# Four fused convolution layers: weights and tables of the small U-net layers loaded once for all groups, with one fold-table buffer fewer

## The chip, the cores and the metric

The kernel runs on one NeuronCore of a Trainium2 chip. A core has four compute engines that run their own instruction streams in order: TensorE (PE, matrix products; PEld is its weight load), VectorE (DVE), ScalarE (ACT) and GpSimd (POOL). SyncE (SP) mostly issues DMA transfers. [...] The metric is the device time of one execution in microseconds (us).

## The reference

The input x is 16 images of 32 channels, 128 x 128, in f32. Four layers follow, each of the form x = x + layer(norm(x)), where the norm takes out mean and variance of pairs of channels.

```python
x = x + _L0_conv_ref(_gn(x), W2, b2, W1, b1)     # row LSTM along diagonals
x = x + _L1_conv_ref(_gn(x), weight)             # out = -sum |patch - w|, 3x3, quantised
x = x + _L2_conv_ref(_gn(x), weights1)           # Hartley transform, 32x32 modes mixed, back
x = x + _L3_conv_ref(_gn(x), ...)                # below

# layer 3
y = get_operator(x)               # five edge operators, each normalised: 160 channels
y = maxpool2(conv3x3(y, conv1))   # 128 -> 64
y = maxpool2(conv3x3(y, conv2))   # 64 -> 32
y = maxpool2(conv3x3(y, conv3))   # 32 -> 16
y = conv3x3(y, conv4)
y = conv3x3(deconv2x2(y, deconv1), conv5)   # 16 -> 32
y = conv3x3(deconv2x2(y, deconv2), conv6)   # 32 -> 64
y = conv3x3(deconv2x2(y, deconv3), conv7)   # 64 -> 128
return orig * y
```

## The kernel before

**Stages.** Stage 0 (layer 0, to about 687 us) runs alone. Then `Differences` makes layer 1 in 32 units (16 images, two halves each). A unit has 72 taps; a tap is one tile of 128 x 8192 values relu(q - w) in f16, made either by DVE (line 760, tile `d_dve`) or by ACT (line 757, tile `d_act`). PE sums each tap over channels (line 647, `acc`). The stage ends near 5616 us, with the last unit.

**Work in the background.** Layers 2 and 3 are made by `After`, in four groups of four images. `After.work` is a generator: `prepare` first, then for each group `forward` (the Hartley transform and the mixing of modes, line 1214), `encoder` (`back`, lines 1278 and 1323; `first_layers`; `small_layers`) and `last` (up7 and the output). Each `yield` tells a planner, `Weave`, what follows: a positive number is so many us of PE work, a negative one a planned wait (for a load, or for DVE), and `("after", 4g+3)` holds group g back until its last image has left layer 1. While `Differences` emits taps, `Weave.advance` emits as much of the generator's work as fits by planned times (a tap is taken as 2.36 us on DVE and 7.15 us on ACT). Whether a tap goes to DVE or ACT, and how many zero products `keep_busy` adds on PE, follows from the same planned times. `keep_order` then fixes that order on every engine.

**After the last unit.** Groups 0 to 2 run in the background of `Differences`, with their tiles on the left side of SBUF. What is left of them when the last unit ends is interleaved with group 3 by `drain`, again by planned times, with planned waits stretched by 1.5 until one of the two is left. Group 3 is done by `end`, a copy of `after` with its tiles on the right, where the layer 1 tiles were, and with more buffers: six for `e_v`.

**`prepare`.** It composes each deconvolution with the convolution that follows into one table (`up5`, `up6`, `up7`, class `Composed`, stored in `up_d`), and for each of the five edge operators a fold table, the `conv1` weights folded with the operator (line 1031 stores it by SP in `fold_d`, 128 x 2880 values; the stores are between 992 and 1325 us).

**`first_layers`.** For each group the mean and variance of the operators' outputs come from Gram products (`statistics`, line 1428). Then the fold tables are weighted with them into one tile of weights, `wf`: ten half tables `v` of 720 KB come by POOL's queue (line 1544), DVE scales the first two (line 1557) and adds the others (line 1559). The pool `e_v` has four buffers: the first four halves are issued inside `statistics`, each further one after the DVE instruction that uses up a buffer. Then `conv1` runs on `wf` (line 1745; the corrections at the picture's rim are line 1780, pooling is line 1672, spreading to the 32-channel layout line 1683), and `small_layers` is called for `conv2`, whose weights are loaded at line 1566.

**`small_layers`, second call.** It makes `conv3`, `conv4` (line 1595), `up5` and `up6` (line 905) of a group of four images. It begins with its loads: `replicated` brings `conv3`'s and `conv4`'s weights (four transfers of 36 KB each, by `by_rows`, line 342), `Composed.loaded` brings a table of 400 KB each for `up5` and `up6` (line 891), all on SP's queue, ten transfers a group; then comes `yield -7.0`. The tiles live in the pool `e_c`, which is opened and closed for each group. `last` loads `up7`'s table in the same way.

**Memory.** Per partition a half table `v` takes 5760 bytes, the weights of one small conv 1152, and one table of `Composed` 3200. POOL's queue has a ring in SBUF, `dynamic_dma_scratch_size`, of 4096 bytes.

Of the kernel before, what the change touches and what calls it, by code (L numbers as in the profile page):

```python
# [333 lines left out]
def by_rows(nc, tile, dram, store=False):  # L334

    for j in range(4):
        part = tile[32 * j : 32 * j + 32]
        rows = bass.AP(dram.tensor, dram.offset + j * dram.ap[0][0], [list(v) for v in dram.ap[1:]])
        if store:
            nc.sync.dma_start(rows, part)  # L340
        else:
            nc.sync.dma_start(part, rows)
# [8 lines left out]
class Weave:  # L351
# [10 lines left out]
    def __init__(self, work):  # L362
        self.work, self.pending = work, None
        self.pe = self.dve = self.act = self.now = self.base = 0.0
        self.until = self.ready = 0.0
        self.draining = self.alone = False
        self.stretch = 1.0
        self.finished, self.count, self.put_off, self.for_act, self.ends = -1, 0, [], [], {}
# [449 lines left out]
def replicated(nc, pool, src, n, name):  # L818

    wr = pool.tile([128, n, 32], F32, name=name)  # L820
    whole = bass.AP(src.tensor, src.offset, [[0, 4], [n * 32, 32], [1, n * 32]])
    by_rows(nc, wr.rearrange("p t o -> p (t o)"), whole)
    return wr
# [135 lines left out]
class After:  # L959


    def __init__(self, nc, tc, side, sm, ps, cst, bias, a, d, stat, out):
        self.nc, self.tc, self.side, self.ps, self.cst, self.bias = nc, tc, side, ps, cst, bias
        self.a, self.d, self.stat, self.out = a, d, stat, out
        self.spare, self.banks = None, 0
        self.sm, self.scales = sm, {}
        self.buffers = {"t_x": 4, "xm": 3, "xw": 2, "t_w": 3, "t_r": 4, "frames": 2, "gm": 5, "e_v": 4, "l_x": 2}
        store = [d["up"][i] for i in range(3)]
        self.up5 = Composed(nc, sm, a, "deconv1", "conv5", bias[:, 7:8], bias[:, 4:5], store[0])
        self.up6 = Composed(nc, sm, a, "deconv2", "conv6", bias[:, 8:9], bias[:, 5:6], store[1])  # L970
        self.up7 = Composed(nc, sm, a, "deconv3", "conv7", bias[:, 9:10], bias[:, 6:7], store[2])
# [25 lines left out]
    def prepare(self):  # L997

        nc, tc = self.nc, self.tc
        with self.pool("p_sm") as pool:  # L1000
            for up in (self.up5, self.up6, self.up7):
                yield from up.compose(pool, self.ps)
        with self.pool("f_sm") as pool:
            w1 = replicated(nc, pool, self.a["conv1"], 45, "w1")
            yield -20.0
            for k, op in enumerate(OPERATORS):
                t = pool.tile([128, 90, 32], F32, name="fold", bufs=2)
                nc.vector.memset(t, 0.0)
                src = w1[:, 9 * k : 9 * k + 9, :].rearrange("p (h w) o -> p h (w o)", w=3)
                for n, (th, tw, r0, c0, h, w, sign) in PARTS.items():  # L1010
                    at, const = PART_AT[n]
                    v = t[:, at : at + h * w, :].rearrange("p (h w) o -> p h (w o)", w=w)
                    for ur in range(3):
                        for uc in range(3):
                            rows = [i for i in th if 0 <= i + ur - r0 < h]
                            cols = [i for i in tw if 0 <= i + uc - c0 < w]
                            if not op[ur][uc] or not rows or not cols:
                                continue
                            r, c = rows[0] + ur - r0, cols[0] + uc - c0
                            dst = v[:, r : r + len(rows), 32 * c : 32 * (c + len(cols))]  # L1020
                            s = src[:, rows[0] : rows[-1] + 1, 32 * cols[0] : 32 * (cols[-1] + 1)]
                            nc.vector.scalar_tensor_tensor(dst, s, sign * op[ur][uc], dst, ALU.mult, ALU.add)
                            self.weave.dve += 0.25
                            yield -1.0
                    for i in th:
                        for j in tw:
                            nc.vector.scalar_tensor_tensor(
                                t[:, const], w1[:, 9 * k + 3 * i + j], -sign, t[:, const], ALU.mult, ALU.add
                            )
                yield SUMMED  # L1030
                nc.sync.dma_start(self.d["fold"][k], t.rearrange("p t o -> p (t o)"))

    def forward(self, g):

# [496 lines left out]
    def first_layers(self, g, fp, frames, y2):  # L1531
        nc, tc, weave = self.nc, self.tc, self.weave
        sides = fp.tile([128, H + 4, 4], F32, name="sides")
        ops = fp.tile([128, 2, 5], F32, name="ops")
        wf = fp.tile([128, 90, 32], F32, name="wf")
        b1 = fp.tile([128, 4], F32, name="b1")
        with self.pool("e_v", self.buffers["e_v"]) as pool:
            v = []

            def table():  # L1540

                k, half = len(v) // 2, len(v) % 2
                v.append(pool.tile([128, 45, 32], F32, name="v"))
                nc.gpsimd.dma_start(
                    v[-1].rearrange("p t o -> p (t o)"), self.d["fold"][k, :, 1440 * half : 1440 * half + 1440]
                )

            with self.pool("e_s") as es:
                yield from self.statistics(g, es, frames, sides, ops, lambda: [table() for _ in range(self.buffers["e_v"])])
            yield -0.5  # L1550
            for n in range(10):
                k, half = n // 2, n % 2
                for part, i in (((0, 81 - 45), 0), ((81 - 45, 45), 1)) if half else (((0, 45), 0),):
                    s = ops[:, i, k : k + 1]
                    to, t = wf[:, 45 * half + part[0] : 45 * half + part[1]], v[n][:, part[0] : part[1]]
                    if k == 0:
                        nc.vector.tensor_scalar(to, t, s, None, ALU.mult)
                    else:
                        nc.vector.scalar_tensor_tensor(to, t, s, to, ALU.mult, ALU.add)
                    weave.dve += 0.1 + 0.033 * (part[1] - part[0])  # L1560
                if len(v) < 10:
                    table()
                yield -1.2
        with self.pool("e_y1") as y1p:
            y1 = self.padded(y1p, 64, "y1")
            self.wc = {"conv2": replicated(nc, y1p, self.a["conv2"], 9, "w_conv2")}
            yield from self.conv1(g, y1p, frames, y1, sides, wf, b1)
            with self.pool("e_c2") as cp:
                yield from self.small_layers(cp, None, y1, y2)

    def small_layers(self, cp, rp, y1, y2):

        nc, tc, weave, bias = self.nc, self.tc, self.weave, self.bias
        wc = self.wc
        if not y1:
            for n in ("conv3", "conv4"):
                wc[n] = replicated(nc, cp, self.a[n], 9, f"w_{n}")
            up5, up6 = self.up5.loaded(cp), self.up6.loaded(cp)
            y3, y4, y5 = (self.padded(cp, n, f"y{i}") for n, i in ((16, 3), (16, 4), (32, 5)))
            self.y6 = y6 = self.padded(rp, 64, "y6")  # L1580
            yield -7.0

        def conv(src, n, name, evict):
            rows = min(n // 4, 512 // n)
# [468 lines left out]
```

## Time and profile before

Four runs took 6645.91, 6638.22, 6632.50 and 6645.64 us, median 6641.93. The profiled execution is the first.

| what | value |
|---|---|
| profiled execution | 6645.91 us, span 6644.1 us |
| stage 0, 0 to 687 us: PE / DVE / ACT busy | 465.8 / 561.5 / 513.3 us |
| taps, 687 to 5616 us: PE / DVE / ACT busy | 4036.2 / 4677.1 / 4745.5 us of 4929 |
| after the last tap, 5616 to 6644 us: PE / DVE / ACT busy | 833.2 / 312.5 / 177.0 us of 1028 |
| mean granted TensorE clock | 0.916 |
| `v` from `fold_d`, POOL's queue | 40 transfers of 720 KB |
| `w_conv`, SP's queue | 48 transfers of 36 KB |
| `u_conv`, SP's queue | 12 transfers of 400 KB |

How to read the profile: it is one execution. "Busy" leaves out waits and the issue of DMA. A group of instructions is given with its source line, its engine, the operation, the tile written and the tiles read, how many there are, and the idle time of the engine just before them with what ended it ("<-DVE d_dve L760" means that a DVE instruction of line 760 released it, "<-DMA v" that a transfer into `v` did, "<-issue" that no wait is seen). The page records most f32 matmuls of `conv1` twice: 25,600 records stand for 12,800 instructions. A clock of 1.0 would be full speed.

### The profile page before, as it was taken

What the parts mean: (1) busy time and instruction counts of PE and PEld (TensorE: products, weight loads), DVE (VectorE), ACT (ScalarE), POOL (GpSimd) and SP (SyncE); (2) the same over time, 40 slices, a digit from 0 to 9 for tenths busy, and PEclk for the clock granted to TensorE, in tenths of its full rate; (3) what the DMA queues carried; (4) which work ended last, traced back from release to release, by engine and by line L of the source; (5) the groups of instructions that cost most, each with busy time, mean ns of one, the idle gap of its engine ahead of it and who ended that gap; (6) DMA issues with size and microseconds to landing.
All of it is one profiled execution on the core that took longest, in us unless ns stands there. A gap on an engine that the chain in (4) does not pass through costs nothing.

```text
span 6644.1 us, 269240 instructions
## 1 busy us (share of the span) xinstructions
PE 5335.2 (80%) x126168; PEld 2775.4 (42%) x126168; DVE 5551.2 (84%) x6858; ACT 5435.8 (82%) x3191; POOL 70.0 (1%) x67
## 2 busy tenths in 40 slices
PE   3698677788777879997887879997877879887796
PEld 3675333334333433333333433333433434454584
DVE  7898899999999999998999999999999998242322
ACT  3898899999999999998999989999999998102112
POOL 0000000000000000000000000000000000000000
PEclk9999899999999989998989889998998889977897
DMA  7553322111344622212553732222553632347304
GB/s 317 212 190 118 79 58 62 53 45 47 75 137 124 195 83 72 56 45 57 118 156 95 214 105 61 56 56 50 123 153 91 196 114 72 119 142 210 94 27 108
DMA packets 380767, 728.06 MB, mean 110 GB/s; under 512 B 73284, under 2 KB 225348, under 8 KB 368772
## 3 DMA queue, kind: packets, MB, share of 16 engines
q1 hardware_dynamic: 372180, 676.41, 35.3%
q0 software_dynamic: 7040, 33.80, 1.5%
q8 instruction: 987, 16.17, 1.0%
q14 instruction: 128, 1.05, 0.1%
q10 hardware_dynamic: 432, 0.64, 0.0%
HBM read 510.69 MB, written 200.00 MB: 107 GB/s over the span
## 4 chain that ended last, share of the span: by engine, by line
issue 33%; PE 31%; DVE 20%; ACT 11%; DMA 3%; SPq 1%; POOL 0%; DVEq 0%; ACTq 0%; POOLq 0%
DVE d_dve L760 12%; PE acc L1745 11%; PE acc L647 9%; ACT d_act L757 8%; PE pg L223 3%; PE acc L905 3%; PE acc L1595 2%; ACT gt L237 2%; DVE y L1683 1%; ACT junk L198 1%; DVE stat L124 1%; PE acc L1428 1%; DVE pooled L1672 1%; DMA xm_d<-xm 1%; ACT th L247 1%
## 5 line engine op out<-in xcount | busy, mean ns | idle before, releaser
L757 ACT ACTIVATE d_act<-q,neg 128x8192 f16<-128x8192 f16 (+1 forms) x626 | 4428.3, 7153 | 164.9 <-PE acc L647 138.5
L760 DVE TENSOR_SCALAR d_dve<-q,qw 128x8192 f16<-128x8192 f16 (+1 forms) x1678 | 3870.8, 2361 | 180.3 <-PE acc L647 160.9
L647 PE MATMUL acc<-d_dve,sel 128*32 128x512 f16 x26848 | 1866.5, 401 | 456.2 <-DVE d_dve L760 353.2
L647 PEld LDWEIGHTS <-sel 128*32 128x32 f16 x36864 | 1003.3, 100 | 2096.7 <-issue 1428.4
L1745 PE MATMUL acc<-xp,wf 32*32 32x512 f32 x25600 | 986.8, 615 | 18.6 <-issue 14.9
L647 PE MATMUL acc<-d_act,sel 128*32 128x512 f16 x10016 | 723.8, 410 | 312.7 <-ACT d_act L757 296.9
L1745 PEld LDWEIGHTS acc<-xp,wf 32*32 32x32 f32 x25600 | 424.6, 104 | 379.6 <-issue 301.1
L1686 ACT ACTIVATE y<-pooled,b 32x128 f32<-32x128 f32 x456 | 182.4, 400 | 430.6 <-DVE pooled L1672 424.4
L905 PE MATMUL acc<-y,u_conv 32*32 32x256 f32 (+1 forms) x9728 | 342.5, 467 | 78.1 <-issue 59.9
L677 PE MATMUL acc<-q,zero 128*32 128x512 f16 x5676 | 402.9, 395 | 0.2 <-issue 0.2
L223 PE MATMUL pg<-h,wb 64*64 64x20 f32 (+15 forms) x8192 | 342.1, 305 | 60.8 <-DVE h L251 34.9
L237 ACT ACTIVATE gt<-pg,bias 128x20 f32<-128x20 f32 (+15 forms) x1024 | 331.7, 383 | 41.4 <-PE pg L223 39.4
L223 PEld LDWEIGHTS pg<-h,wb 64*64 64x64 f32 x8192 | 252.2, 150 | 136.1 <-DVE h L251 82.3
L1428 PE MATMUL acc<-xp 32*64 32x204 f32 (+3 forms) x8576 | 251.8, 345 | 53.8 <-issue 53.7
L905 PEld LDWEIGHTS acc<-y,u_conv 32*32 32x32 f32 x9728 | 154.5, 111 | 207.2 <-issue 158.3
L1844 ACT ACTIVATE xr<-xr,l_ms 128x1024 f32<-128x1024 f32 x64 | 68.7, 1146 | 209.5 <-DVE xr L1874 158.9
L1780 DVE TENSOR_TENSOR acc<-acc,cut 128x4 f32<-128x4 f32 x256 | 36.3, 165 | 234.6 <-PE acc L1745 231.9
L677 PEld LDWEIGHTS <-zero 128*32 128x32 f16 x5676 | 168.4, 100 | 152.3 <-issue 24.9
L1428 PEld LDWEIGHTS acc<-xp 32*64 32x64 f32 (+1 forms) x8576 | 171.2, 134 | 144.6 <-issue 139.6
L1373 ACT ACTIVATE xp<-xp,shift,stats 128x1280 f32<-128x1280 f32 (+1 forms) x64 | 91.5, 1434 | 161.2 <-DVE shift L1341 110.6
L1874 DVE SCALAR_TENSOR_TENSOR xr<-acc,l_one,xr 128x512 f32<-128x512 f32 x128 | 87.6, 743 | 155.8 <-PE acc L905 135.7
L223 PE MATMUL pg<-xn,wb 64*64 64x2 f32 (+63 forms) x4096 | 184.5, 290 | 24.5 <-issue 14.3
(217 smaller groups left out, 3739.9 us busy)
## 6 DMA issues: line engine op xcount, KB each, us to landing
q<-q_d SPq DMA_DIRECT2D x128, 536.2 KB, 9.6
xp<-xn_d SPq DMA_DIRECT2D x64, 660.0 KB, 4.9
xp<-x_d SPq DMA_DIRECT2D x56, 640.0 KB, 5.9
xr<-xn_d SPq DMA_DIRECT2D x64, 528.0 KB, 11.9
x_in<-in_x_dram SPq DMA_DIRECT2D x16, 2048.0 KB, 14.7
xn<-in_xs_dram SPq DMA_DIRECT2D x64, 512.0 KB, 7.0
res<-in_x_dram SPq DMA_DIRECT2D x64, 512.0 KB, 8.7
x_d<-res SPq DMA_DIRECT2D x64, 512.0 KB, 4.8
```

The lines of the kernel that those rows point to most:

```text
L223: nc.tensor.matmul(bank[c][q][64 * pair : 64 * pair + 64, :, :width], wb[half, 4 * kind + KIND[q]].rearrange("p b o -> p (b o)"), v[half], ...
L237: nc.scalar.activation(gt[:, q, :, :n], bank[c][q][:, :, :n], AF.Tanh if q == G else AF.Sigmoid, bias=bias[:, KIND[q] : KIND[q] + 1],)
L647: self.nc.tensor.matmul(acc[k][32 * j : 32 * j + 32, :], self.sel16[:, i // 9, :], d[:, row : row + 4, c : c + W], start=first, stop=last,)
L677: self.nc.tensor.matmul(acc[k][32 * j : 32 * j + 32, :], self.zero, q[:, :4, :W], start=False, stop=False)
L757: nc.scalar.activation(dst, src, AF.Relu, bias=self.neg[:, i : i + 1])
L760: nc.vector.tensor_scalar(dst, src, self.qw[:, i : i + 1], 0.0, ALU.subtract, ALU.max)
L905: nc.tensor.matmul(acc[blk][32 * j : 32 * j + 32, o : o + rows * n], t[part, 4 * par + tap, :], src[part, top : top + rows, left : left + ...
L1373: nc.scalar.activation(v, v, AF.Identity, bias=self.shift3, scale=self.stats3[:, 1])
L1428: nc.tensor.matmul(gram[blk][j : j + width, at : at + n], xp[part, l, 2 + j : 2 + j + width], xp[part, rows, j : j + width + 4], start=sta ...
L1595: nc.tensor.matmul(acc[blk][32 * j : 32 * j + 32, : rows * n], wc[name][part, tap, :], src[part, at : at + rows, kw : kw + n], start=tap == 0,
L1686: nc.scalar.activation(d, s, AF.Identity, bias=bj)
L1745: nc.tensor.matmul(acc[blk][32 * j : 32 * j + 32, :], tap_of("all", tap)[rows], xp[rows, 4 * j + kh : 4 * j + kh + 4, kw : kw + W], start= ...
```

## The change

- The weights of `conv3` and `conv4` and the tables of `up5` and `up6` are loaded at the end of `prepare` into the pool `sm`, which lives for the rest of the program: ten transfers on SP's queue, once, behind the store of the last fold table. All four groups use these tiles (`end` is a copy of `after` and shares them).
- `small_layers` has no loads of its own any more, and its planned wait is 1.0 in place of 7.0.
- `e_v` has three buffers for groups 0 to 2 in place of four. Group 3 keeps six.
- `dynamic_dma_scratch_size` is 2048 in place of 4096.

Per partition that is 8704 bytes more for the tables, 5760 less for `e_v` and 2048 less for the ring.

```diff
@@ After.__init__
-        self.buffers = {"t_x": 4, "xm": 3, "xw": 2, "t_w": 3, "t_r": 4, "frames": 2, "gm": 5, "e_v": 4, "l_x": 2}
+        self.buffers = {"t_x": 4, "xm": 3, "xw": 2, "t_w": 3, "t_r": 4, "frames": 2, "gm": 5, "e_v": 3, "l_x": 2}
@@ After.prepare, at its end
                 nc.sync.dma_start(self.d["fold"][k], t.rearrange("p t o -> p (t o)"))
+        self.wc = {n: replicated(nc, self.sm, self.a[n], 9, f"w_{n}") for n in ("conv3", "conv4")}
+        self.ups = self.up5.loaded(self.sm), self.up6.loaded(self.sm)
@@ After.first_layers
-            self.wc = {"conv2": replicated(nc, y1p, self.a["conv2"], 9, "w_conv2")}
+            self.wc["conv2"] = replicated(nc, y1p, self.a["conv2"], 9, "w_conv2")
@@ After.small_layers
         if not y1:
-            for n in ("conv3", "conv4"):
-                wc[n] = replicated(nc, cp, self.a[n], 9, f"w_{n}")
-            up5, up6 = self.up5.loaded(cp), self.up6.loaded(cp)
+            up5, up6 = self.ups
             y3, y4, y5 = (self.padded(cp, n, f"y{i}") for n, i in ((16, 3), (16, 4), (32, 5)))
             self.y6 = y6 = self.padded(rp, 64, "y6")
-            yield -7.0
+            yield -1.0
@@ kernel
-    nc = bacc.Bacc("TRN2", target_bir_lowering=False, num_devices=1, dynamic_dma_scratch_size=4096)
+    nc = bacc.Bacc("TRN2", target_bir_lowering=False, num_devices=1, dynamic_dma_scratch_size=2048)
```

The order of the built programs differs as follows. SP has 2346 instructions in place of 2376. DVE makes 1676 taps in place of 1678 and ACT 628 in place of 626. PE has 5860 zero products in place of 5676. All other counts are the same. The order is the same up to group 0's small layers, but for the ten loads and the fold-table reloads; from there the background work comes some taps earlier.

## The prediction

> **What bounds the kernel now.** I read the busy times first, then the table of stretches, then single pieces of the timeline at the two places where the change reorders work: the fold tables of groups 0 to 2, and the stretch after the last tap.
>
> ```profile
> PE 5335.2 (80%) x126168; PEld 2775.4 (42%) x126168; DVE 5551.2 (84%) x6858; ACT 5435.8 (82%) x3191; POOL 70.0 (1%) x67
> L757 ACT ACTIVATE d_act<-q,neg 128x8192 f16<-128x8192 f16 (+1 forms) x626 | 4428.3, 7153 | 164.9 <-PE acc L647 138.5
> L760 DVE TENSOR_SCALAR d_dve<-q,qw 128x8192 f16<-128x8192 f16 (+1 forms) x1678 | 3870.8, 2361 | 180.3 <-PE acc L647 160.9
> ```
>
> Three engines look alike over the whole span, so no single one "is" the bound. The stretches tell more (length; busy us and instructions of PE, weight loads, DVE, ACT, POOL; granted clock; DMA share; GB/s):
>
> ```profile
> 3054.00:5616.00 2562.00, 2111.84 (x49099) 977.36 (x49114) 2408.42 (x2102) 2442.65 (x660) 38.13 (x30) 0.91 0.40 108
> 5616.00:5749.00 133.00, 112.19 (x2560) 51.97 (x2528) 42.26 (x138) 22.17 (x48) 0.00 (x0) 0.95 0.53 165
> 5749.00:5830.00 81.00, 73.74 (x2647) 41.47 (x2648) 9.39 (x41) 12.87 (x32) 0.00 (x0) 0.92 0.28 85
> 5901.00:6005.00 104.00, 83.73 (x1524) 50.67 (x1534) 76.84 (x202) 5.70 (x9) 5.80 (x11) 0.64 0.73 238
> ```
>
> While taps run (the first row is its second half, to 5616), DVE idles 2562 − 2408 = 154 us and ACT 119 us: both are full, so DVE or ACT work added there costs time, and PE work (idle 450 us) is free. After the last tap, from 5616 to 6644, PE leads: what is taken off PE there shortens the end, unless a wait takes its place.
>
> **Part 1: the tail (the likely gain).** The planner no longer leaves 7 planned us per group for loads; group 0's small layers start 6 to 7 taps earlier, and this head start grows into group 2. In the built programs, 192 matmuls of group 2's `conv1` (12 conv taps of 16) now stand ahead of the last tap's sums instead of behind them.
>
> ```profile
> 5620.60 12.06 PE L1745 MATMUL acc<-xp,wf 32*32 32x512 f32 x365
> 5749.14 1.88 PE L1214 MATMUL acc<-xs,mix 128*32 128x8 f32 x124 [16.11 <-DVE acc L1780]
> 5821.95 2.57 SPq L1264 DMA_DIRECT2D zi<-z_d  x4
> 5829.58 1.26 PE L1278 MATMUL acc<-cw,zi 32*32 32x32 f32 x78
> 5931.48 2.39 DVE L1683 TENSOR_SCALAR y<-pooled,bias 32x128 f32<-32x128 f32 x8
> 5934.78 3.82 SPq L342 DMA_DIRECT2D w_conv<-in_conv_dram  x8
> 5938.56 2.11 PE L1595 MATMUL acc<-y,w_conv 32*32 32x256 f32 x36 [10.41 <-DMA w_conv<-in_conv_dram]
> 5940.60 2.66 PE L1323 MATMUL acc<-cw,o 32*128 32x128 f32 x16
> ```
>
> (Start, length, engine, line, tiles, count; in brackets the idle time before and what ended it.)
>
> *A1, −12.7 us.* A matmul leaves two records here. The first line has 365 records in 12.06 us, 0.033 each, so 0.066 us a matmul; 192 × 0.066 = 12.7. They move under the taps, where PE has 450 us idle.
>
> *A2, −14.5 us.* In the second line PE stands 16.11 us before group 3's first mode product. Between the last forward product and that point the program before has 112 `conv1` matmuls, the changed one 384 (80 of them came from ahead of it, 192 from behind). The way from that forward product to the mode product takes 112 × 0.066 + 16.1 = 23.5 us; 384 × 0.066 = 25.3 us of work cover it. I leave a tenth of the wait, 1.6 us: −14.5. Bounds: −16.1, and −3.4 where only the 192 from behind count for nothing (16.1 − 192 × 0.066): the mode products then gain no pace from the work taken out between them.
>
> *A3, −4.7 us.* PE waits 10.41 us for `conv3`'s weights, to 5938.56. Its other input is ready at 5931.48 + 2.39 = 5933.87. Without the load the wait ends there: 4.7 us. SP's ten issues leave this place with it. Bounds 0 and −4.7: less is gained where SP's queue is late anyway.
>
> *A4, +9.7 us.* A new wait. From the last mode product (ends 5814.4) to the first product on `zi` (5829.58) z is stored and loaded back, 15.2 us; 224 `conv1` matmuls of group 2 fill PE meanwhile, 80 in the changed program: 80 × 0.066 = 5.3 us, with the 0.2 us of gaps in that stretch 5.5. 15.2 − 5.5 = 9.7. Bounds 0 (the store goes out in parts, and the earlier parts are back sooner) and 12.6 (half of the 80 stand too early).
>
> *A5, +3 us.* Two rounds of `up6` of group 2 stand in front of group 3's Gram statistics in the new order. Each needs 6.12 us on DVE and about as much on ACT for its spreads, and DVE is busy 76.84 of 104 us in that stretch (last row above). A quarter of 12 shows: 3; bounds 0 and 12.
>
> [...]
>
> Sum of the tail: −12.7 − 14.5 − 4.7 + 9.7 + 3 = −19.2 us; from −33.5 (A2 whole, no A4, no A5) to +8.5 (A2 −3.4, A3 0, A4 12.6, A5 12).
>
> **Part 2: under the taps (the likely loss).** *B1, +2 us.* The 192 matmuls bring 16 spreads of y1 onto ACT, 0.41 us each (y1 rows of this trace), 6.6 us of ACT. DVE makes a tap in 2.36 us and ACT in 7.15, together 0.563 a us; ACT's 6.6 us are 0.92 taps, 1.6 us of both; I take 2.
>
> *B2, +5 us.* Groups 0 to 2 keep three buffers for the ten half tables instead of four.
>
> ```profile
>   DMA to landing us min/median/max: 4.3/7.1/14.2
> 2377.94 5.10 DVE L1559 SCALAR_TENSOR_TENSOR wf<-v,ops,wf 128x1440 f32<-128x1440 f32 x4
> 3915.48 5.27 DVE L1559 SCALAR_TENSOR_TENSOR wf<-v,ops,wf 128x1440 f32<-128x1440 f32 x4 [7.02 <-DMA v<-fold_d]
> ```
>
> A table's buffer is free when DVE has used it; POOL then issues the reload (0.9 us to wake and issue), it lands after L, and two more tables of 1.7 us and on average 0.9 tap of 2.27 us lie in between: 5.4 us of cover. A round of three tables so waits L + 0.9 − 5.4. Seven reloads are 7/3 rounds, times three groups 7: 7L − 31.5. Today's stalls go with it: 7.0 in group 1 (the last line), 0.3 + 1.3 in group 2, none in group 0. What is added is 7L − 40.1. Fastest landing 4.3: nothing waits, −8.6. Group 0's and 2's medians 6.3 and 7.0: +4 and +9. Group 1's slow reloads, 13.8: +56.5. I take +5, near group 0's, since the tables stand in two of three groups at those loads; DVE's wait costs fully because ACT fills only its own taps.
>
> [...]
>
> *B3, 0.* SP loses 24 loads of 36 KB and 6 of 400 KB and gains 10 once, behind the last table's store near 1324 us; they land in 2 to 4 us, and the first reader runs near 3062. Their queue is SP's; its next load of x has ten taps of slack (24 us). If that slack is gone: 10 × 4 = 40 us at most, which nothing here suggests. *B4, 0.* The smaller ring matters to POOL's 67 transfers alone: an issue takes 0.53 us or 2.09 today; if every reload took the longer, 1.56 × 7 = +11.
>
> Sum under the taps: +7; the new order alone may shift taps by some 12 us either way (8% of DVE's 154 idle us).
>
> **The sum.** −19.2 + 7 = −12.2. The profiled run took 6645.9 us (span 6644.1): 6633.7. It lies 4.0 above the median of the four runs (6641.93), so 6630 after rounding. A difference below 0.2%, 13.3 us, can't be told from none here.
>
> **Rivals.** *The head start counts in full:* z comes back in time (A4, A5 nothing). For it: `zi` today loads behind full cover. Against: 80 records are too short for 15.2 us. −31.9 + 2 + 4 = −26; 6645.9 − 26 − 4 = 6616.
> *The tail doesn't follow PE:* group 3's own chain of DMA and DVE steps sets the end, and group 2's moved work was only filling. For it: PE is idle 147 us in the tail, and group 3's loads of the same weights are hidden already (PE waits for DVE's y at 6479, not for weights), so the change doesn't do there what it says. Against: PE is busy 91% from 5749 to 5830. Only A3 is left: −4.7 + 7 = +2, 6644.
> *Slower: the reloads govern DVE.* Three buffers make each round of tables as long as a landing. For it: the stall at 3915 with four. Against: none in group 0. By 7L − 40.1 and the other −17.2, the gain is gone at a mean landing of 8.2 us, and from 10.1 it is slower by over 13.3. At 11: +19.5, 6661; at 13.8: +39, 6681.
>
> **Chances.** Forecast 0.42 (0.27 faster, 0.14 same, 0.01 slower); head start in full 0.17, faster; tail doesn't follow 0.24 (0.14 same, 0.10 slower); reloads govern 0.17 (0.02 same, 0.15 slower). Faster 0.44, same 0.30, slower 0.26. The forecast's own range is 6614 to 6646 (the sum with the replan noise of 12 and 4 more either way for B2). For 8 in 10 the range reaches from 6602, the full head start with a lucky replan (6616 − 12, rounded), to 6661, reloads at 11 us.
>
> **What would show it.** A1: the last tap's sum to the first `zi` product is shorter. A2: no 16 us idle before the first L1214 of group 3. A3: no PE wait on `w_conv` in the tail. A4: an idle of some 9 us before L1278 after `zi`. A5: DVE late at the Gram products. B2: waits "<-DMA v" in front of L1557 and L1559, 18 us over three groups if L is 7. I am wrong if the tail (last tap to end) is within 5 us of 1028, or if table waits exceed 30 us.

## The result and the profile after

The changed kernel takes 6652.37 us (median of 31 runs, 6639.4 to 6666.76) against 6640.5 us before (51 runs, 6624.97 to 6654.39). The ratio is 1.0017, 95% interval [1.0012, 1.0022]: slower by 11 us by the ratio and 12 by the medians. That is less than the 0.2% below which the prediction would see no difference, but the interval doesn't reach 1, and the way is not the one that was forecast. The profiled execution took 6655.81 us with a span of 6653.8, 9.7 us over that of before.

The page of the changed kernel shows the busy times, and the two groups that make the taps (busy us, mean ns | idle us before them, what ended it):

```profile
PE 5350.4 (80%) x126352; PEld 2782.3 (42%) x126352; DVE 5545.1 (83%) x6856; ACT 5451.6 (82%) x3193; POOL 69.1 (1%) x67
...
L757 ACT ACTIVATE d_act<-q,neg 128x8192 f16<-128x8192 f16 (+1 forms) x628 | 4444.3, 7145 | 141.9 <-PE acc L647 118.6
L760 DVE TENSOR_SCALAR d_dve<-q,qw 128x8192 f16<-128x8192 f16 (+1 forms) x1676 | 3865.3, 2360 | 210.8 <-PE acc L647 190.9
```

DVE is busy 6 us less than before, yet it idles 211 us in front of its taps where it idled 180: it waits 30 us more for PE to sum a tap and free the tile. ACT makes two taps more and DVE two fewer: ACT is busy 16 us more and idles 142 us in front of its taps instead of 165. The stretches say where (length; busy us and count of PE, weight loads, DVE, ACT, POOL; clock; DMA share; GB/s): second half of the taps, then the tail to the mode products, the mode products to `zi`, the Gram phase's start.

```profile
3052.00:5637.00 2585.00, 2127.39 (x49319) 981.11 (x49309) 2398.52 (x2093) 2458.61 (x674) 37.60 (x30) 0.91 0.39 107
5639.00:5788.00 149.00, 129.49 (x2975) 65.04 (x2948) 44.81 (x148) 23.01 (x50) 0.00 (x0) 0.93 0.50 153
5788.00:5850.00 62.00, 49.25 (x1858) 21.96 (x1858) 9.05 (x41) 8.26 (x21) 0.00 (x0) 0.84 0.26 75
5922.00:6026.00 104.00, 90.77 (x1864) 54.53 (x1858) 83.09 (x194) 11.70 (x18) 5.79 (x11) 0.66 0.64 197
```

The second half of the taps is 2585 us long instead of 2562, with DVE idle 186 us instead of 154 and no more DVE work. From the first tap to the start of the last instruction of line 628, which finishes the last unit, the *tap stage* below, it is 4960.1 us against 4934.9: +25.2. From there to the end, the *tail*, it is 1008.7 against 1022.0: −13.3. What was won behind the taps was lost nearly twice over under them.

Two pieces of the tail's timeline of the changed kernel answer to the waits quoted before (start, length, engine, line, tiles, count [idle before]); line numbers from 1032 to 1577 are two higher here:

```profile
5754.70 0.17 DVE L1188 COPY xw<-xs 64x32 f32<-64x32 f32 x1 [14.76 <-DMA xw<-xm_d]
...
5755.85 0.23 DVE L1780 TENSOR_TENSOR acc<-acc,cut 128x4 f32<-128x4 f32 x2
...
5756.64 1.29 DVE L1672 TENSOR_REDUCE pooled<-acc 128x128 f32<-128x512 f32 x2
...
5757.43 30.54 PE L1745 MATMUL acc<-xp,wf 32*32 32x512 f32 x768 [14.26 <-issue]
...
5849.66 0.28 PE L1280 MATMUL acc<-cw,zi 32*32 32x32 f32 x2 [4.44 <-DMA zi<-z_d]
...
5945.25 4.08 PE L1595 MATMUL acc<-y,w_conv 32*32 32x256 f32 x32 [2.35 <-DVE pooled L1672]
```

The 16.11 us wait didn't go. It stands as 14.26 us in front of the very `conv1` block (768 records) that was to fill it. DVE stands 14.76 us on the load of the modes, `xw`, and behind that in its queue are the rim correction (line 1780) and the pooling (line 1672), which read `conv1`'s last accumulators and free them. In the kernel before DVE stood there too, for longer:

```profile
5736.99 0.17 DVE L1186 COPY xw<-xs 64x32 f32<-64x32 f32 x1 [19.32 <-DMA xw<-xm_d]
```

The `zi` wait of the changed kernel is 4.44 us, and the wait on `conv3`'s weights has become 2.35 us on pooling.

### The profile page after: what moved, and what is told of

It reads as the page before. It is cut to its first block, busy times and chain, and to the rows that moved or that the text cites. A ratio compares the mean times of both kernels' runs of the same rounds, so it can differ in the third digit from the quotient of the medians.

```text
span 6653.8 us, 269560 instructions
## 1 busy us (share of the span) xinstructions
PE 5350.4 (80%) x126352; PEld 2782.3 (42%) x126352; DVE 5545.1 (83%) x6856; ACT 5451.6 (82%) x3193; POOL 69.1 (1%) x67
## 4 chain that ended last, share of the span: by engine, by line
PE 32%; issue 30%; DVE 21%; ACT 14%; DMA 2%; SPq 1%; DVEq 0%; POOL 0%; ACTq 0%; POOLq 0%
DVE d_dve L760 13%; PE acc L1745 11%; ACT d_act L757 10%; PE acc L647 9%; PE acc L905 3%; PE pg L223 3%; PE acc L1430 2%; PE acc L1595 2%; ACT gt L237 2%; DVE y L1683 1%; ACT junk L198 1%; DVE stat L124 1%; DMA x_in<-in_x_dram 1%; ACT th L247 1%; DVE pooled L1672 1%
## 5 line engine op out<-in xcount | busy, mean ns | idle before, releaser
L677 PE MATMUL acc<-q,zero 128*32 128x512 f16 x5860 | 420.0, 399 | 0.0
L1780 DVE TENSOR_TENSOR acc<-acc,cut 128x4 f32<-128x4 f32 x256 | 36.0, 164 | 199.5 <-PE acc L1745 197.0
L1595 PE MATMUL acc<-y,w_conv 32*32 32x512 f32 (+2 forms) x4608 | 173.7, 529 | 33.4 <-issue 14.3
```

The costliest lines, as they stand in the source:

```text
L677: self.nc.tensor.matmul(acc[k][32 * j : 32 * j + 32, :], self.zero, q[:, :4, :W], start=False, stop=False)
L1595: nc.tensor.matmul(acc[blk][32 * j : 32 * j + 32, : rows * n], wc[name][part, tap, :], src[part, at : at + rows, kw : kw + n], start=tap == 0,
```

## The experiments

One profile gives the stages of each run; the ratio to the kernel before comes from the timed runs. The runs were made in sets on several chips, on which the kernel before took 6637.6 to 6652.8 us in the median, so ratios are compared and not times. "Stops" are breaks of over 1.8 us that PE makes, in the tap stage, between two products of the same line with the same tiles while the profile shows no wait: their number, and us in total. "Behind stops" is DVE's idle time of over 0.5 us before a tap that overlaps such a stop or begins within 6 us of its end; "other" is the rest of such idle time, without the 16 us in front of the first tap. (The expectations of e9 and e10 count 5 to 10 us more as behind stops, since they take in places where PE itself waits for a tap.)

| kernel | ratio, 95% interval | tap stage | tail | stops | behind stops | other |
|---|---|---|---|---|---|---|
| before | | 4934.9 | 1022.0 | 20, 69 | 72 | 77 |
| after | 1.0017 [1.0012, 1.0022] | 4960.1 | 1008.7 | 22, 85 | 97 | 87 |
| e1 hoist, wait 7 | 1.0003 [0.9993, 1.0013] | 4935.9 | 1022.6 | 16, 52 | 51 | 88 |
| e2 wait 1 only | 1.0011 [1.0002, 1.0020] | 4962.7 | 1011.4 | 31, 105 | 109 | 77 |
| e3 wait 1 in the tail | 0.9996 [0.9987, 1.0006] | 4931.2 | 1025.6 | 17, 57 | 56 | 79 |
| e4 buffers and ring | 1.0013 [1.0003, 1.0023] | 4938.2 | 1031.7 | 18, 60 | 64 | 82 |
| e5 wait 6 | 1.0003 [0.9992, 1.0015] | 4935.0 | 1034.3 | 20, 69 | 59 | 84 |
| e6 wait 16 | 1.0007 [0.9998, 1.0017] | 4947.3 | 1013.1 | 18, 58 | 59 | 92 |
| e7 (order of after) | 1.0014 [1.0005, 1.0024] | 4962.2 | 1015.7 | 28, 98 | 108 | 71 |
| e8 (order of before) | 1.0002 [0.9992, 1.0012] | 4921.6 | 1035.6 | 22, 71 | 66 | 73 |
| e9 after, spread loads | 0.9994 [0.9984, 1.0004] | 4951.6 | 999.0 | 22, 76 | 67 | 107 |
| e10 before, spread loads | 0.9978 [0.9969, 0.9987] | 4915.1 | 1026.3 | 22, 76 | 54 | 88 |
| e11 wait 4 | 1.0039 [1.0027, 1.0052] | 4958.5 | 1019.0 | 24, 83 | 84 | 97 |
| e12 hoist, wait 7, spread | 0.9980 [0.9971, 0.9989] | 4930.6 | 1020.6 | 18, 63 | 54 | 97 |

**First question: order, or memory?** e1 is the changed kernel with the wait put back:

```diff
-            yield -1.0
+            yield -7.0
```

> The changed kernel with the planned wait put back to 7.0, so that the order of the taps and the background work is that of before; hoisted loads, three fold buffers and the small ring stay. If the 25 us lost under the taps come from the new order: the last tap ends as before (near 5622 us), the weight wait of group 2 in the tail is shorter by some 5 us, about 6636 us. If they come from three buffers, the small ring or the hoisted loads: the last tap ends near 5640 to 5647 and the time is 6650 to 6662.

e2 is the kernel before with the wait alone:

```diff
-            yield -7.0
+            yield -1.0
```

> The kernel before with the planned wait of 1.0 alone; loads per group, four fold buffers and the ring of 4 KB stay. If the order is the cause: the last tap ends near 5645 as in the changed kernel, and the products of conv3 wait for their weights besides (5 to 10 us a group), 6652 to 6665. If memory and loads are the cause: the taps end near 5622 and only the tail is shorter, near 6630.

e3 is the changed kernel with the new wait only behind the taps:

```diff
-            yield -1.0
+            yield -1.0 if weave.draining else -7.0
```

> The changed kernel with the wait of 1.0 only where the work is drained after the last tap, and 7.0 under the taps. If the order under the taps is the cause: taps end near 5622, group 2's conv3 starts 5 us sooner and the planned wait of the tail is gone, 6628 to 6637. If memory is the cause: taps end near 5645, 6645 to 6655.

e4 is the kernel before with the two memory edits:

```diff
-"e_v": 4
+"e_v": 3
-dynamic_dma_scratch_size=4096
+dynamic_dma_scratch_size=2048
```

> The kernel before with three fold buffers and the ring of 2 KB alone, no table hoisted. If the order is the cause: as before within 5 us, 6636 to 6645. If the reloads of the fold tables are the cause: taps end 10 to 25 us late with waits on v of 15 us and more, 6650 to 6665.

The tap stage answers plainly. With the order of before it is 4935.9, 4931.2 and 4938.2 us whatever the memory; with the order of the shorter wait it is 4962.7, though e2 hoists nothing and keeps four buffers. So the loss under the taps comes with the order. (The timed ratios alone would not say so: e4, with the order of before, has 1.0013 and e2 1.0011.) e2 still waits 8.2 us for `conv3`'s weights in the tail, and its tail is as short as the changed kernel's: removing that load isn't what shortens the tail. e1 and e3 missed their expected gain of 5 us and more: the weight wait is gone in e1 and the Gram products begin 378.1 us after the last unit's end instead of 383.6, but they end at 525.3 instead of 524.1. e4's ratio is above 1 by a little, and its Gram products end some 10 us later; but so do those of e8, which has none of the memory edits, and e1 and e3 hold e4's two edits without a loss in the ratio. So e4's 1.0013 is not settled.

The fold tables in the same runs (DVE's waits on `v` over the tap stage: us in total, times, longest). First the kernel before, then e1, then the changed kernel:

```profile
DVE wf L1559 <- DMA v<-fold_d: 7.4, 2, 7.0
```

```profile
DVE wf L1561 <- DMA v<-fold_d: 18.1, 8, 11.3
```

```profile
DVE wf L1561 <- DMA v<-fold_d: 6.7, 8, 2.0
```

Three buffers do wait more where the order stays, by 10.7 us, and not in the changed kernel's order. The number of taps between the tables isn't the reason: it is 3, 3 and 2 in both orders. In the order of before the tables of group 1 run into the load of the next q (e1: q is issued at 3894.7, and the wait of 11.3 us ends at 3911.8); in the changed order they are done at 3888, 15 us ahead of it. In neither case does the tap stage follow these waits.

**Second question: is it the shorter wait, or a new order as such?** e5 and e6 replace `yield -1.0` by `yield -6.0` and `yield -16.0`, both of which make a new order under the taps.

> The changed kernel with a planned wait of 6.0, another order of taps and background work. If the shorter wait itself delays the taps (PE reaches conv3 too early and holds the tap sums up): nearly as with 7.0, the taps take 4935 us from the first to the end, at most 4 more. If any new order scatters the tap stage: 4925 to 4965, with no relation to the length of the wait.

> The changed kernel with a planned wait of 16.0, so no wait is shorter than before and the order is new. If the shorter wait itself delays the taps: 4935 us or less for the tap stage. If any new order scatters it: 4925 to 4965.

With 6 the tap stage is 4935.0, with 16 it is 4947.3, though no wait is shorter there. The length of the wait alone doesn't order the results. Five profiles with the order of before lie between 4921.6 and 4938.2 (mean 4932), three with the order of the changed kernel between 4960.1 and 4962.7, so 4947 lies outside both.

Two things on record bear on the shorter wait. ACT's two taps more aren't the cause: e5 splits the taps in the same way (1676 and 628), with nearly as many zero products (5796 against 5860), and takes 4935.0 us. But something of the loss does belong to the wait's length. In front of `conv4`'s results in group 0 and 1 (line 1683) DVE waits for PE 12.1 us in the changed kernel, 12.0 in e2, 11.4 in e7 and 13.2 in e11 with its wait of 4, against 1.1 to 3.8 in the five profiles with the order of before, 6.6 with a wait of 6 and 3.2 with 16. That is some 9 us of DVE on top of the 30 in front of taps. Waits of 1 and 4 both give a long tap stage, 6 and 7 a short one, so that too short a wait delays the taps isn't ruled out; that any new order scatters is shown by the 16 alone, in one profile.

**Third question: the wait for the modes in the tail.** The edit was to delay four of six transfers of mode weights in the tail, in e7 on the changed kernel and in e8 on the one before:

```diff
-wt = [self.weights(wp, i) for i in range(self.buffers["t_w"])]
+wt = [self.weights(wp, i) for i in range(2 if weave.draining else self.buffers["t_w"])]
...
+while len(wt) < self.buffers["t_w"]:
+    wt.append(self.weights(wp, len(wt)))
 yield from self.mixing(g, xs, wp, wt)
```

> The changed kernel, and after the last tap only two of the six 1 MB mode weights are issued ahead of the planned wait, the other four behind the last modes' additions; PE and DVE keep the order of the changed kernel. If the 14 us before the moved conv1 block are DVE standing on the modes' load behind those six transfers: the idle time falls to 3 to 8 us, the first mode product comes 6 to 11 us sooner, and the tail shrinks by as much only if group 3's chain carries it through the Gram products. If DVE's wait has another cause: no difference, 14 us stay.

> The kernel before with the same split of the mode weights. If DVE's 19 us wait on the modes' load is made by the six transfers: it falls under 10 us, the first mode product comes 8 to 13 us sooner than 127 us after the last unit's end, and the tail falls from 1022 us by up to that. Otherwise no difference.

The built programs keep the order on every engine and on SP: six transfers still stand together ahead of the last modes' store. So e7 and e8 don't test the six transfers. The traces of the two kernels show where the time goes all the same: the last store of modes (`xm_d`), issued right behind the six, lands 17.2 us after its issue before and 13.6 us after the change, while the stores ahead of the six take 1.8 to 2.7 us, and SP issues the loads of the modes as it has landed, at 5733.63 and 5751.31 us. As repeats of the two orders e7 and e8 show how far one profile goes: the same order as before gives 4921.6 + 1035.6 instead of 4934.9 + 1022.0, the changed one 4962.2 + 1015.7 instead of 4960.1 + 1008.7.

**Fourth question: what does PE wait for while the taps wait for PE?** Where DVE idles 5 us and more before a tap in the changed kernel, PE has stopped in the middle of a block of equal products, in wait of nothing that the profile shows (11 of 11 such places). One of these places, PE and DVE:

```profile
4718.36 0.67 PE L905 MATMUL acc<-y,u_conv 32*32 32x256 f32 x18
...
4724.01 1.10 PE L905 MATMUL acc<-y,u_conv 32*32 32x256 f32 x14 [4.98 <-issue]
...
4725.04 3.37 PE L647 MATMUL acc<-d_dve,sel 128*32 128x512 f16 x32
...
4726.99 2.38 DVE L760 TENSOR_SCALAR d_dve<-q,qw 128x8320 f16<-128x8320 f16 x1 [6.15 <-PE acc L647]
```

```profile
4719.00:4724.00 5.00, 0.03 (x5) 0.00 (x0) 1.84 (x1) 5.00 (x3) 0.00 (x0) 0.72 1.01 205
```

A block of 32 equal products breaks after 18, for 4.98 us. The sums of two DVE taps stand behind it, DVE's three tiles are full, and it idles 6.15 us. Meanwhile (the row of the stretch) the 16 DMA engines are full, share 1.01: loads of the next images are under way. At another place, the rim products of group 1 (line 1719, 640 records), SP has just issued the next q, four transfers of 550 KB:

```profile
3903.64 2.94 SPq L342 DMA_DIRECT2D q<-q_d  x4
3906.67 12.14 SPq L342 DMA_DIRECT2D xr<-x_d  x8
...
3923.59 0.41 PE L1719 MATMUL acc<-sides,wf 32*32 32x32 f32 x30 [5.62 <-issue]
...
3925.89 2.39 DVE L760 TENSOR_SCALAR d_dve<-q,qw 128x8320 f16<-128x8320 f16 x1 [8.80 <-PE acc L647]
```

The stretch of these products in the order of before, where q came 30 us ahead of them, and in the changed order (columns as above):

```profile
3929.00:3951.00 22.00, 20.82 (x840) 11.88 (x833) 21.53 (x11) 19.66 (x4) 0.00 (x0) 0.85 0.14 37
```

```profile
3895.00:3930.00 35.00, 20.84 (x836) 11.77 (x817) 19.88 (x16) 24.26 (x5) 0.00 (x0) 0.61 0.56 126
```

PE is busy for the same 20.8 us, but takes 35 us instead of 22, with the DMA share at 0.56 instead of 0.14. DVE is busy 19.9 us of 35, against 21.5 of 22.

Taken over the second half of the taps, stops of over 2.5 us (10 before, 13 after) fall where the mean DMA share is 0.79 and 0.80, against 0.40 and 0.39 on the whole.

What comes with the end of a stop can be read from the traces. The page of before lists a queue of "instruction" transfers, 987 packets of 16.17 MB, so 16,384 bytes each; there are 252,336 records on PE and PEld, 256 for each packet in the mean. What a packet holds, no view shows. In the stop shown above, PE breaks off at 4719.03. The DMA queues from 4719 to 4721, and from 4721 to 4722 (packets, MB, share of the 16 engines):

```profile
q1 hardware_dynamic: 108, 0.42, 96.0%
```

```profile
q1 hardware_dynamic: 57, 0.19, 96.1%
q8 instruction: 1, 0.02, 8.6%
```

The one instruction packet starts at 4721.04 and is done at 4722.41; PE goes on 1.60 us later. So it is everywhere: each of the 298 stops in the 14 profiles ends between 1.20 and 1.78 us after the end of such a packet, while a moment taken at random in the tap stage lies so in 8% of the cases. That PE lacks its next instructions until then is the author's reading of these times; no trace shows it directly. The 86 stops during which the DMA share is under 0.3 take 2.4 us in the mean, the other 212 take 3.8. So stops came with little DMA too, and were 1.4 us longer in the mean where the engines were busier.

Whether other transfers make the stops, and with them the loss, is what e9 and e10 try: they spread the loads of a unit, while PE, DVE and ACT keep their order.

```diff
-if i == 8 and (b, half) != (B - 1, 1):
-    following = self.loaded(b + half, 1 - half)
+if i in (8, 14, 20, 26) and (b, half) != (B - 1, 1):
+    following = self.loaded(b + half, 1 - half, (i - 8) // 6, following if i > 8 else None)
-if i == 40:
-    unit["xr"] = self.residual(b, half)
+if i in (38, 46):
+    unit["xr"] = unit.get("xr", []) + self.residual(b, half, i // 46)
```

Here `loaded` issues the one block of 32 partitions that it is told, and `residual` one of its two tiles.

> The changed kernel with each unit's loads spread out: the four row blocks of the next q (550 KB each) are issued 6 taps apart instead of all at tap 8, the two residual tiles at taps 38 and 46 instead of both at 40. PE, DVE and ACT keep the changed kernel's order. If the lost time is PE standing in the middle of a block while transfers keep the DMA engines busy, with the taps' sums queued behind it: those stops move or shorten, DVE's tap idle behind them falls from about 110 us towards 70, and the tap stage from 4961 us to 4920 to 4945. If the order of PE, DVE and ACT alone makes the loss: 4955 to 4968.

> The kernel before with the same spread loads. If bursts of transfers make PE's stops: DVE's tap idle behind them falls from about 68 us to 40 to 60 and the tap stage from 4922 to 4938 down to 4900 to 4925. If bursts have no part: unchanged.

Both kernels gain about as much: from 1.0017 to 0.9994, and to 0.9978, 15 us each of 6640. In e9 the stops take 76 us instead of 85 and 98, DVE's idle behind them falls from 97 and 108 us to 67, the tap stage from 4960 and 4962 to 4952, less than was expected, and the rest of DVE's idle grows to 107. In e10 the stops aren't shorter, 76 us against 52 to 71 in the five profiles with the same order. Its tap stage, 4915.1, is the shortest of all but within 7 us of e8's. The place shown above is, in e9 (line numbers are four higher):

```profile
4716.33 0.67 PE L909 MATMUL acc<-y,u_conv 32*32 32x256 f32 x18
...
4720.30 1.10 PE L909 MATMUL acc<-y,u_conv 32*32 32x256 f32 x14 [3.30 <-issue]
```

The same block breaks at the same product, for 3.30 us instead of 4.98. Part of e9's gain shows as a shorter tail, for which the edit gives no reason. So that spreading the loads helps is shown by the timed ratios; that it helps by shorter stops isn't.

e11 is the changed kernel with `yield -4.0`:

> The changed kernel with a planned wait of 4.0: another order under the taps than with 1.0, and the same 192 conv1 products ahead of the last tap's end. If what is moved under the taps costs there what it saves: tap stage 4955 to 4965 and tail 1008 to 1016 as with 1.0. If the loss under the taps is a matter of where PE's stops fall in that order: tap stage 4925 to 4950, tail 1008 to 1018, and the time falls under the kernel before by up to 15 us.

It gave 4958.5 and 1019.0 us, and 1.0039, the slowest of all. The better of the two expected outcomes failed; but it falls behind the kernel before in the same units as the changed kernel (units 20, 24, 26 and 28, counted from 0, by 20, 12, 13 and 20 us there against 10, 12, 11 and 21; both win 18 to 19 us back in each of units 27 and 29), and its stops take 83 us. It is no independent draw, and doesn't tell a price of the moved work from the fall of the stops.

e12 puts e1 and the spread loads together:

> The changed kernel with the planned wait of 7.0 and the spread loads: hoisted tables, three fold buffers, small ring, the order of before. If hoisting is worth nothing while the order stays: as the kernel before with spread loads, ratio 0.997 to 0.999 to before. If the early tables shorten the tail once bursts are spread: under 0.997. If the extra waits on the fold tables (18 us in all against 7) cost their length: 0.9985 to 1.0000.

0.9980 against e10's 0.9978: with order and loads equal, the hoisted tables are worth nothing that these runs can show. Against e1, 1.0003, it is a third pair in which spreading is worth 0.2%. e10 and e12 beat both kernels.

## Why the prediction was wrong

The text forecast 6630 and put 0.44 on faster; the kernel became slower by 0.17%. The time lies inside the wide range that was given, but not for a reason of the forecast. The failed step is the last line of part 2: "the new order alone may shift taps by some 12 us either way". It stands in the sum with nothing, and was sized as 8% of DVE's idle time, as scatter around zero. The orders of before and of the change differ by 29 us in the tap stage (means of five and three profiles). That the order makes this is shown by e1, e2 and e3. By what way is shown in part. PE's stops take 96 us on the mean of after, e2 and e7, against 62 for before, e1, e3, e4 and e8, and DVE's idle behind them 105 against 62, while the rest of DVE's idle before taps is 71 to 88 in all eight. PE work was called free there ("idle 450 us"), but at 4719 us, shown above, the block of background work broke off for 4.98 us, the sums of two DVE taps stood behind it in PE's order, and DVE, with its three tiles full, idled 6.15 us. The planner knows no stops and can't place them. Why one order has more of them than another is open, and they aren't all: e6 has stops of 58 us and a tap stage of 4947.

The prediction's own signs of being wrong looked elsewhere: from the last tap to the end it is 1015 us, not within 5 of 1028, and the waits on tables are 6.7 us, not over 30.

*A1 and A2* (−27.2 together). The 192 products did move, but the mode products, the spectral layer's end and the Gram products' end come hardly sooner: the last Gram product starts 524.1 us after the last unit before and 525.0 in the changed kernel, and over all 524 to 536 in the five profiles with the order of before and 525 to 532 in the three of the change. A2's reason failed: the wait's releaser in the quoted row was "DVE acc L1780", an instruction of `conv1` itself, queued behind DVE's wait of 19.32 us on the modes. More `conv1` work can't cover a wait that holds `conv1`'s own accumulators. The rival "the tail doesn't follow PE" is right as far as the Gram products' end.

*A3* (−4.7). The wait on weights is gone, 5.5 us at the Gram products' start, and nothing at their end: hidden, the rival's view again, against the rival's own sum, which kept it.

*A4* (+9.7). There is a new wait and it is 4.44 us, since z is back in 10.1 us instead of 15.2. A4 counts no slower clock, and little of one showed: the granted clock behind the new wait is 0.56 from 5850 to 5855 us and 1.00 from there to 5880, where before, behind the wait of 10.41 us, it was 0.50 from 5939 to 5964. *A5* (+3). From first to last Gram product 147.0 us instead of 140.5, but e1, with the order of before, has 147.2: not told apart.

Even so the tail is shorter by 13 to 20 us, and all of it lies behind the Gram products: from their end to the end of the kernel 497.9, 499.6, 497.3 and 496.5 us (before, e8, e1, e4) against 483.7, 483.7 and 481.7 (after, e7, e2). There PE is the busiest engine: 400 of 498 us before and 385 of 484 in the changed kernel. What went is PE's work, 15 us, and its idle time stayed, 97 and 98 us. Of the products of line 905 with 256 columns 3200 records stand there instead of 3456: 128 products of group 2's `up7` were moved ahead. So work taken off PE did shorten the end here, by 14 us for 15, as the prediction held, but it isn't the `conv1` work of A1. That −19.2 came near the tail's −13.3 was luck: it came by other steps than those named.

*B1* (+2): ACT's busy time beside the taps in the tap stage is 323 us in both kernels, not 6.6 more; what ACT got instead is two taps, 16 us. *B2* (+5): the rule 7L − 40.1 gives 10 us at the median landing of 7.1, and 10.7 were measured in e1 with the order of before; in the changed order the waits on `v` are 0.7 us shorter than before. The slower rival, reloads that govern DVE, didn't come. *B3* and *B4* (0): e1 holds both and can't be told from the kernel before.

Three figures of the prediction are slips that carry nothing: PE's idle time in the tail is 1028 − 833 = 195 us, not 147; 6616 − 12 is 6604, not 6602; and SP loses 32 loads of 36 KB and 8 of 400 KB and gains 10, where the text counts the 10 twice.

## What to carry to other kernels

A change that shortens a planned wait in a kernel whose order is planned is, above all, a new order: price it by the spread of neighbouring orders (here 0 to 30 us in the tap stage) before the terms that are argued, and separate the two by a run that keeps the old order. PE's idle time wasn't free for work in the background here: DVE idled 105 us behind PE's stops in the mean of the changed order and 62 in that of before, while PE idled 450 us in the stage's second half before. When idle time is to be filled, read which instruction ends it, and whether the filler needs that same instruction. Where an engine stops without a wait, look when the packets of the instruction queue come (here 1.20 to 1.78 us before the end of each of 298 stops).

## What the runs showed of the hardware

PE broke off in the middle of blocks of equal products for 1.8 to 7 us at a time, 16 to 31 times in a tap stage, 52 to 105 us in all; a block of line 905 broke after the same 18 records of 32 in the changed kernel and in e9. The instruction queue moved packets of 16,384 bytes, in the kernel before one for 256 records of PE and PEld in the mean, and all 298 stops ended 1.20 to 1.78 us after the end of such a packet. They were longer where the DMA engines were busier (3.8 us in the mean, against 2.4 where their share was under 0.3). Spreading 2.2 MB of loads over 18 taps instead of issuing them at once took 0.2% off in three pairs of kernels. What a packet holds, why one comes when it does, and whether the spreading works through the packets, is not shown.
